# Moving work between VectorE, ScalarE and GpSimd in a macaron block with a chunked delta-rule attention, under a new order of instructions

## The chip, the cores and the metric

The kernel runs on one core of a Trainium2 chip. The time is the device time of one execution in microseconds, from the start of the program to its end; lower is better. The engines are TensorE (PE; PEld is its weight load), VectorE (DVE), ScalarE (ACT), GpSimd (POOL) and SyncE (SP), which issues the DMAs.

## The reference

The input x has 8 sequences of 256 rows and 256 channels. Three residual steps are applied to it:

```python
x = x + 0.5 * ffn(layernorm(x))
x = x + attn(layernorm(x))
x = x + 0.5 * ffn(layernorm(x))
```

The feed-forward part is a gated unit of 1024 with Hadamard transforms, which the kernel folds into the weights. The attention has 16 heads, each with a key and value width of 128. For every row there are one query and R = 4 key/value pairs, taken from projections that run through a causal convolution of 4 taps and a SiLU; q and k are normalized; a decay per row and channel comes from a softplus (G is its running sum). The sequence is cut into chunks with a state S of 128x128 carried from one to the next:

```python
w = beta * k
M[t,i; s,m] = sum_d k[t,i] * exp(G[t] - G[s]) * w[s,m]     # strictly lower triangular
rhs = v - (k * exp(G)) @ S
u = solve(I + M, rhs)                                        # unit diagonal
o = SCALE * (q * exp(G) @ S + tril(q * exp(G[t] - G[s]) @ w) @ u)
S = exp(G_last) * S + (w * exp(G_last - G)).T @ u
...
out = (o * rsqrt(mean(o**2) + eps) * onorm_w * sigmoid(gate)) @ Wo.T
```

## The kernel before

There are three stages: the first feed-forward with the gate inputs, the attention, and the output projection with the second feed-forward. Nearly all of the time is the attention stage, and all of the change is there but for a constant.

The attention stage works on 64 groups: 4 pairs of sequences (bp; the two sequences of a pair are b = 0 and 1) times 16 heads, in this order. The kernel uses chunks of C = 32 rows, 8 for each sequence. The steps of one group:

- `proj` (L946): nine projections of 128x512 (one for q, four for k, four for v). Each is six matmuls in TensorE; ScalarE writes the last convolution tap into kr or vr, and VectorE adds the other three. In the 16 groups of bp = 0 the weights are also split into high and low parts (wblk, a cast on ScalarE, a subtraction on GpSimd) and stored; later groups fetch them (w_d).
- `silu_k` (L1012) writes kq (SiLU, 128x1280 for each b) and copies the keys into k4; `silu_v` (L998) writes v4 (SiLU, 128x1024 for each b) and sig (Tanh).
- `gates` (L1025): the softplus (za, zm: Abs, Relu, Exp, Ln on ScalarE), the scan cs on VectorE, then the decays of five levels in el: subtractions on GpSimd, one Exp on ScalarE for each b. Level lv serves pairs of blocks of 2^lv rows. ek, eg, qh and nq come from the same scan.
- `m_piece` (L1094), four pieces pc for each group: the products of keys and decays (l0, l1, ls2 to ls4 for the columns, lt1 to lt4 for the rows), then 160 small matmuls into a PSUM tile mt for each half piece, from which N (ScalarE) and at (VectorE) are read.
- `inverse` (L1187): the 32x32 diagonal blocks of N go to DRAM (nd) and come back, one block for each partition (nl); GpSimd solves all columns at once in 31 steps of a product (ltmp) and a sum (yl). nk, the norms of the keys, is a square root: a power on GpSimd. The result goes through DRAM (yd) into Yt.
- `double` (L1238) makes 128x128 inverses of the 32x32 ones: VectorE transposes blocks (Xt), a 32-row step (p32, copy ps1, y32), and a 64-row step (p64, copy ps2, y64, copy into Yt).
- `recur` (L1385): for 8 chunks and both sequences p_r (TensorE), rt (VectorE), p_u (TensorE), u (copy), p_s (TensorE), S (VectorE), with ke, kd, kdT, vN prepared by `recur_prep` (L1304).
- `post` (L1400): rs, the reciprocal root for the normalization, a power on GpSimd; the scaling of o, its transposes, the product with sig and the store.

**The order.** Every operation is recorded first. `arrange` (L402) then sorts the operations of all groups by group x period + a position that the table ROUND (L41) holds for the operation's kind and number; each engine gets its instructions in that order, once and for all. Positions of one group reach from about -100 to 190 while the period is 68.814, so a round of the machine holds work of four groups: the projections of a later one, the pieces of the next, the inverse, and the recurrence of an earlier one. A position modulo the period gives the place in a round. BUFS (L37) has the number of buffers for each tile, ENG (L39) the engine of each copy and product (v VectorE, g GpSimd, s ScalarE), one letter for each instance.

**Tables of ScalarE.** `act` (L226) names the table set that a function needs. While `arrange` goes through the order, it puts in a table load wherever an operation needs another set than the last one: SILU_SET for v4, sig (Tanh) and kq, EXP_SET for the Exp and Ln of za, el and ek. Copies, Abs, Relu, Square and scalings name none.

**Fillers.** `keep_warm` (L582) puts matmuls on constants (L1454, into a spare part of mt) into planned gaps of TensorE, as long as the planned busy share of the last 3.4 us is below BUSY.

Of the kernel before, what the change touches and what calls it, by code (L numbers as in the profile page):

```python
# [20 lines left out]
P = 128  # L21
# [15 lines left out]
BUFS = {'kr': 1, 'vr': 1, 'kq': 2, 'v4': 4, 'k4': 5, 'N': 8, 'at': 9, 'ek': 4, 'eg': 6, 'qh': 4, 'wblk': 2, 'w2': 1, 'sm': 3, 'cl': 2, 'nk': 3, 'nq': 16, 'sig': 3, 'so': 24, 'rs': 21, 'ke': 3, 'kd': 1, 'vN': 2, 'kdT': 3, 'u': 8, 'S': 8, 'rt': 2, 'ps2': 1, 'wraw': 2, 'f_h': 8, 'raw': 3, 'ohl': 3, 'x4': 1, 'f_xhl': 1, 'ln_xn': 1, 'xhl': 1, 'fg': 1, 'be': 1, 'za': 1, 'zm': 1, 'el': 1, 'q2': 2, 'l0': 1, 'lt1': 1, 'lt2': 1, 'ls2': 1, 'lt3': 1, 'ls3': 1, 'lt4': 1, 'ls4': 2, 'nl': 1, 'sw': 1, 'yl': 1, 'ltmp': 1, 'ps1': 1, 'o': 1}  # L37

ENG = {'l0': 'vvvv', 'l1': 'vvvg', 'lt1': 'vvvv', 'lt2': 'gvvv', 'lt3': 'vvvv', 'lt4': 'vvvv', 'ls2': 'vvvv', 'ls3': 'vvvv', 'ls4': 'vvvv', 'ke': 'vvvvvvvv', 'kd': 'vvvvvvvv', 'qh': 'vv', 'k4': 'ss', 'zm': 'v', 'nl': 'v', 'el': 'gggggggggg', 'ek': 'gg', 'N': 'ssssssss', 'u': 'ssssssssssssvsss', 'vN': 'ssssssssssssssss', 'kdT': 'ssssssss', 'ps1': 'ssss', 'ps2': 'ss', 'X32': 'ss', 'Y32': 'ssss', 'Y64': 'ss', 'o': 'ssss', 'on': 'ssss', 'nk': 's', 'eg': 'ss', 'wh': 's', 'at': 'vvvvvvvv', 'tap': 'vvvvvvvvv'}  # L39

ROUND = {"period": 68.814, "at": {  # L41
    'gp:ek': [11.377, 12.737],
    'gp:el': [-25.595, -25.712, -24.539, -25.433, -23.461, -25.598, -23.752, -23.755, -25.592, -23.755, 9.204, 4.916, 8.065, 5.102, 6.615, 4.377, 9.811, 4.773, 10.026, 10.591],
    'gp:l1_1': [28.618],
    'gp:lt2': [-22.399],
    'gp:ltmp': [48.887, 51.825, 53.362, 54.257, 54.649, 56.717, 61.287, 62.202, 64.383, 64.837, 66.74, 67.664, 69.55, 73.202, 73.876, 76.049, 78.203, 78.703, 79.577, 81.108, 81.477, 85.569, 88.294, 89.684, 90.649, 91.459, 91.894, 93.63, 93.767, 96.173, 96.359],
    'gp:nk': [98.248],
    'gp:rs': [173.727],
    'gp:wblk': [-90.104, -89.629, -67.446, -59.41, -57.936, -40.937, -38.162, -32.75, -28.503],
    'gp:yl': [34.532, 47.962, 48.222, 49.996, 52.065, 53.571, 54.563, 55.066, 60.271, 61.711, 63.621, 64.509, 66.1, 67.039, 68.097, 71.874, 73.69, 74.124, 76.947, 78.452, 79.147, 79.975, 81.426, 85.281, 85.934, 89.07, 90.329, 91.062, 91.866, 93.407, 93.652, 95.846, 96.181, 96.554],  # L50
    'sc:N': [-6.953, -7.892, 11.221, 16.582, 21.323, 26.437, 31.718, 35.019],
    'sc:Xt0': [113.673],
    'sc:Xt1': [113.782],
    'sc:Yt0': [115.328, 114.885, 117.841],
    'sc:Yt1': [115.453, 115.214, 118.518],
    'sc:eg': [86.088, 108.103],
    'sc:ek': [17.438, 13.205, 17.438, 17.441],
    'sc:el': [-23.061, 10.712],
    'sc:k4': [-25.428, 9.155],
    'sc:kdT': [97.137, 101.186, 129.746, 130.662, 140.024, 143.13, 151.489, 157.263],  # L60
    'sc:kq': [-31.991, -31.802],
    'sc:kr': [-68.822, -62.007, -59.973, -50.065, -48.956],
    'sc:nk': [67.803],
    'sc:o': [147.184, 143.199, 151.16, 165.94, 165.972, 167.312, 176.914, 178.906, 176.92, 176.569],
    'sc:ps1': [110.606, 110.094],
    'sc:ps2': [115.551, 117.509],
    'sc:q2': [-10.36, 22.442],
    'sc:sig': [26.085],
    'sc:u': [119.942, 123.611, 127.068, 129.495, 136.818, 138.35, 141.509, 141.948, 146.735, 147.631, 149.124, 154.215, 161.784, 165.023, 165.068],
    'sc:v4': [27.91, 28.253],  # L70
    'sc:vN': [100.738, 100.735, 101.434, 101.213, 127.78, 127.071, 129.587, 130.228, 141.392, 141.576, 141.945, 142.52, 150.948, 156.786, 156.382, 155.345],
    'sc:vr': [-34.884, -28.219, -27.02, -20.568],
    'sc:wblk': [-91.119, -90.691, -67.582, -64.336, -59.106, -49.023, -40.507, -35.493, -28.927],
    'sc:za': [-33.996, -31.044, -30.853],
    'sc:zm': [-34.081],
    'sy:Yt0': [105.729, 107.105, 104.757, 107.387],
    'sy:Yt1': [103.524, 106.806, 103.662, 107.727],
    'sy:be': [44.808, -20.372],
    'sy:fgl': [-45.079],
    'sy:nd': [4.23, 16.805, 16.828, 17.812, 18.974, 19.369, 22.319, 27.202, 30.032, 30.711, 32.382, 34.581, 36.972, 38.357, 40.801, 41.422],  # L80
    'sy:nl': [43.757, 43.901],
    'sy:o': [186.894],
    'sy:w': [-89.684, -87.074, -66.467, -51.713, -42.051, -38.245, -35.074, -25.824, -26.322],
    'sy:w2': [-41.765],
    'sy:wblk': [-93.367, -89.838, -67.181, -66.47, -52.1, -43.986, -38.28, -30.869, -30.06],
    'sy:wraw': [-92.729, -91.457, -89.183, -87.864, -65.109, -49.447, -41.511, -37.744, -30.244],
    'sy:xhl': [-93.404],
    'sy:yd': [99.135, 100.159],
    'te:mt0': [-10.644, 0, 0, 0, 0, 0, 0, 0, 0, 0, 0, 0, 0, 0, 0, 0, 0, 0, 0, 0, 0, 0, 0, 0, 0, 0, 0, 0, 0, 0, 0, 0, 0, 0, 0, 0, 0, 0, 0, 0, 0, 0, 0, 0, 0, 0, 0, 0, 9.442, 0, 0, 0, 0, 0, 0, 0, 0, 0, 0, 0, 0, 0, 0, 0, 0, 0, 0, 0, 0, 0, 0, 0, 0, 0, 0, 0, 0, 0, 0, 0, 0, 0, 0, 0, 0, 0, 0, 0, 0, 0, 0, 0, 0, 0, 0, 0, 19.694, 0, 0, 0, 0, 0, 0, 0, 0, 0, 0, 0, 0, 0, 0, 0, 0, 0, 0, 0, 0, 0, 0, 0, 0, 0, 0, 0, 0, 0, 0, 0, 0, 0, 0, 0, 0, 0, 0, 0, 0, 0, 0, 0, 0, 0, 0, 0, 28.864],
    'te:mt1': [-17.993, 0, 0, 0, 0, 0, 0, 0, 0, 0, 0, 0, 0, 0, 0, 0, 0, 0, 0, 0, 0, 0, 0, 0, 0, 0, 0, 0, 0, 0, 0, 0, 0, 0, 0, 0, 0, 0, 0, 0, 0, 0, 0, 0, 0, 0, 0, 0, 11.4, 0, 0, 0, 0, 0, 0, 0, 0, 0, 0, 0, 0, 0, 0, 0, 0, 0, 0, 0, 0, 0, 0, 0, 0, 0, 0, 0, 0, 0, 0, 0, 0, 0, 0, 0, 0, 0, 0, 0, 0, 0, 0, 0, 0, 0, 0, 0, 24.906, 0, 0, 0, 0, 0, 0, 0, 0, 0, 0, 0, 0, 0, 0, 0, 0, 0, 0, 0, 0, 0, 0, 0, 0, 0, 0, 0, 0, 0, 0, 0, 0, 0, 0, 0, 0, 0, 0, 0, 0, 0, 0, 0, 0, 0, 0, 0, 34.527],  # L90
    'te:p32': [108.88],
    'te:p64': [115.408, 0, 0, 0, 0, 0, 0, 0, 116.095],
    'te:p_ot': [179.18],
    'te:p_r': [124.617, 126.108, 133.994, 136.571, 139.4, 140.262, 144.848, 145.843, 148.38, 148.537, 156.119, 157.599, 162.507, 162.792],
    'te:p_s': [122.138, 123.878, 127.286, 130.259, 137.699, 139.056, 142.425, 143.6, 147.291, 148.063, 149.938, 156.545, 158.406, 162.504],
    'te:p_u': [119.002, 121.356, 126.433, 127.195, 136.764, 137.598, 140.805, 141.927, 146.259, 147.258, 148.54, 152.195, 157.045, 159.754, 163.073, 164.034],
    'te:pgate': [22.588],
    'te:pn': [67.727],
    'te:po': [142.529, 0, 0, 0, 0, 0, 0, 0, 0, 0, 0, 0, 0, 0, 165.6],
    'te:pproj': [-76.39, 0, 0, -70.897, 0, 0, -67.676, 0, 0, -66.718, 0, 0, -61.594, 0, 0, -60.722, 0, 0, -57.959, 0, 0, -54.182, 0, 0, -49.585, 0, 0, -49.501, 0, 0, -37.337, 0, 0, -35.82, 0, 0, -32.624, 0, 0, -31.701, 0, 0, -29.108, 0, 0, -27.327, 0, 0, -25.906, 0, 0, -25.514],  # L100
    'te:pq': [37.003, 38.263, 37.124, 37.775],
    'te:pv': [90.502, 0, 94.616, 0, 101.112, 0, 101.115, 0, 125.899, 0, 122.248, 0, 118.999, 0, 126.094, 0, 137.287, 0, 137.412, 0, 141.79, 0, 141.625, 0, 148.543, 0, 148.383, 155.095, 0, 152.784],
    'te:pz': [-35.014],
    'te:y32': [111.675],
    'te:y64': [117.131, 0, 0, 0, 0, 0, 0, 0, 117.578],
    've:S': [123.037, 124.889, 130.671, 134.218, 138.442, 139.928, 142.468, 145.226, 147.734, 148.401, 152.826, 156.972, 158.65, 162.627],
    've:Xt0': [107.37, 111.673, 106.836],
    've:Xt1': [105.404, 111.622, 106.244],
    've:at': [0.188, 3.648, 19.324, 19.334, 20.927, 28.353, 42.532, 42.462],
    've:cl': [46.296, 46.593],  # L110
    've:cs': [-29.476],
    've:kd': [90.977, 97.203, 105.267, 124.194, 128.516, 138.134, 144.363, 148.513],
# [7 lines left out]
    've:ls4': [-23.029, -11.997, 13.582, 21.025],  # L120
    've:lt1': [-21.795, -8.666, 19.293, 26.201],
    've:lt2': [-1.993, 19.19, 26.204],
    've:lt3': [-21.792, -5.389, 19.261, 26.774],
    've:lt4': [-22.417, 0.248, 19.314, 27.204],
    've:nl': [46.988],
    've:nq': [39.479],
# [1469 lines left out]
```

## Time and profile before

| | |
|---|---|
| median of 3 runs | 4800.92 us (4788.68 to 4819.71) |
| profiled execution | 4781.15 us, span 4779.4 us |
| granted TensorE clock, mean | 0.951 |
| busy: PE, DVE, ACT, POOL | 4197.5, 3828.0, 3156.2, 3019.2 us |
| first and last scan cs | 272.9 and 4348.1 us |
| DMA | 351.13 MB, mean 73 GB/s |

All instructions of the attention stage are recorded by one helper (L623), so the profile's groups are told apart by the tiles that they write and read and by shapes. "l_g" is l0, "l" is l1, "ls_g" ls2 to ls4, "lt_g" lt1 to lt4, "k_g" k4, "v_g" v4, "ps_g" ps1 and ps2, "p_g" p32 and p64, "y_g" y32 and y64. Durations in a group are means; the idle time in front of a group is put down to what ended it.

### The profile page before, as it was taken

How to read it: one execution, taken by the hardware profiler on the slowest of the kernel's cores; microseconds unless marked ns; L12 is line 12 of the kernel's file. 1: busy time of each engine (PE TensorE's matmuls, PEld its weight loads, DVE VectorE, ACT ScalarE, POOL GpSimd, SP SyncE). 2: the span in 40 equal slices, each digit the busy share in tenths (PEclk: the TensorE clock that was granted, in tenths of full speed). 3: DMA queues.
4: the chain of work that ended last, by engine and by line, in shares of the span. 5: the costliest groups of instructions: out<-in, count | busy, mean ns of one | idle time of the engine just before them, and what ended most of it. 6: DMA issues, size and time to landing. Idle time of an engine off the chain costs nothing.

```text
span 4779.4 us, 197459 instructions
## 1 busy us (share of the span) xinstructions
PE 4197.5 (88%) x83786; PEld 3450.4 (72%) x83786; DVE 3828.0 (80%) x8811; ACT 3156.2 (66%) x7152; POOL 3019.2 (63%) x6090
## 2 busy tenths in 40 slices
PE   8878888888888888888888888888988888888799
PEld 5767777777777777777777777777777777777688
DVE  4368888888888888888988889888889988887333
ACT  3247766776777776777777767777777777776332
POOL 4257776777766667666666676666667766666321
PEclk9989999898999999999999999999999999999899
DMA  3133222322322322223323222223322222222421
GB/s 129 59 103 82 80 74 80 85 71 76 93 75 67 71 61 63 66 67 71 82 68 71 61 64 66 67 68 75 77 61 65 70 65 68 68 66 46 128 85 45
DMA packets 607651, 351.13 MB, mean 73 GB/s; under 512 B 439472, under 2 KB 510896, under 8 KB 605360
## 3 DMA queue, kind: packets, MB, share of 16 engines
q1 hardware_dynamic: 606768, 338.50, 27.6%
q8 instruction: 659, 10.80, 0.9%
q14 instruction: 224, 1.84, 0.1%
HBM read 232.94 MB, written 105.38 MB: 71 GB/s over the span
## 4 chain that ended last, share of the span: by engine, by line
DVE 42%; PE 32%; ACT 13%; DMA 5%; issue 4%; POOL 3%; SPq 1%; POOLq 0%; DVEq 0%; ACTq 0%
DVE kr_g L623 10%; DVE lt_g L623 5%; ACT v_g L623 5%; PE pproj_g L623 4%; DVE S_g L623 4%; PE mt L623 3%; PE p_g L623 3%; DVE ke_g L623 3%; DVE vr_g L623 3%; DVE ls_g L623 3%; DVE rt_g L623 3%; PE y_g L623 3%; PE mt L1454 3%; DMA wblk_g<-w_d 2%; DVE l_g L623 2%
## 5 line engine op out<-in xcount | busy, mean ns | idle before, releaser
L623 PE MATMUL pproj_g<-xhl_g,wblk_g 128*128 128x512 f32 x3456 | 1087.3, 434 | 151.7 <-DMA wblk_g<-w_d 74.1
L623 POOL TENSOR_TENSOR yl_g<-yl_g,ltmp_g 128x126 f32<-128x126 f32 (+22 forms) x1984 | 899.2, 453 | 127.4
L623 POOL TENSOR_TENSOR ltmp_g<-yl_g,nl_g 128x126 f32<-128x126 f32 (+22 forms) x1984 | 815.1, 411 | 121.3 <-POOL yl_g L623 0.3
L623 POOL TENSOR_TENSOR el_g<-cs_g 128x128 f32<-128x128 f32 x1280 | 513.6, 421 | 461.6 <-DVE nq_g L623 437.8
L623 PEld LDWEIGHTS pproj_g<-xhl_g,wblk_g 128*128 128x128 f32 x3456 | 603.4, 197 | 274.0 <-DVE Xt L623 45.8
L623 DVE SCALAR_TENSOR_TENSOR kr_g<-pproj_g,small,kr_g 128x510 f32<-128x510 f32 (+2 forms) x960 | 701.7, 737 | 18.9 <-ACT kr_g L623 15.5
L623 DVE SCALAR_TENSOR_TENSOR vr_g<-pproj_g,small,vr_g 128x510 f32<-128x510 f32 (+2 forms) x768 | 554.2, 735 | 158.6 <-ACT vr_g L623 151.9
L623 ACT COPY u_g<-p_u_g 128x128 f32<-128x128 f32 x960 | 255.7, 266 | 419.0 <-PE p_u_g L623 413.2
L623 DVE TENSOR_TENSOR lt_g<-kq_g,el_g 128x320 f32<-128x320 f32 x960 | 527.3, 580 | 0.0
L623 PE MATMUL mt<-lt_g,ls_g 128*16 128x20 f32 (+2 forms) x16384 | 500.8, 205 | 9.1 <-DVE ls_g L623 1.1
L623 PE MATMUL p_r_g<-S_g,ke_g 128*128 128x128 f32 x1792 | 392.9, 301 | 67.4 <-DVE S_g L623 60.2
L623 ACT ACTIVATE vN_g<-pv_g,nk_g 128x128 f32<-128x128 f32 x1024 | 355.5, 373 | 89.2 <-DVE rt_g L623 80.7
L623 PEld LDWEIGHTS p_r_g<-S_g,ke_g 128*128 128x128 f32 x1792 | 278.5, 189 | 151.4 <-DVE S_g L623 58.4
L623 PE MATMUL p_s_g<-u_g,kdT_g 128*128 128x128 f32 x1792 | 374.9, 291 | 14.5 <-ACT u_g L623 6.7
L623 PE MATMUL p_u_g<-rt_g,Yt 128*128 128x128 f32 x1792 | 373.6, 290 | 12.1 <-DVE rt_g L623 4.4
L623 DVE TENSOR_TENSOR ls_g<-k_g,el_g 128x256 f32<-128x256 f32 x768 | 356.8, 465 | 21.6 <-ACT el_g L623 15.9
L623 PEld LDWEIGHTS p_s_g<-u_g,kdT_g 128*128 128x128 f32 x1792 | 286.7, 192 | 98.1 <-issue 42.0
L623 PE MATMUL mt<-kq_g,k_g 128*32 128x20 f32 x8192 | 308.4, 193 | 38.5 <-DVE at_g L623 38.5
L623 ACT ACTIVATE kr_g<-pproj_g,small 128x512 f32<-128x512 f32 x320 | 219.9, 687 | 160.7 <-PE pproj_g L623 160.7
L623 PEld LDWEIGHTS mt<-lt_g,ls_g 128*16 128x16 f32 (+1 forms) x16384 | 313.7, 102 | 16.5 <-DVE ls_g L623 16.2
L623 PEld LDWEIGHTS p_u_g<-rt_g,Yt 128*128 128x128 f32 x1792 | 273.6, 190 | 68.3 <-DVE rt_g L623 32.7
L623 PEld LDWEIGHTS mt<-kq_g,k_g 128*32 128x32 f32 x8192 | 211.5, 109 | 146.6 <-issue 63.4
(170 smaller groups left out, 10773.4 us busy)
## 6 DMA issues: line engine op xcount, KB each, us to landing
wblk_g<-w_d SPq DMA_DIRECT2D x432, 256.0 KB, 2.9
w_d<-wblk_g SPq DMA_DIRECT2D x144, 256.0 KB, 2.1
nl_g<-nd_g SPq DMA_DIRECT2D x128, 256.0 KB, 4.1
wraw_g<-in_wa_dram SPq DMA_DIRECT2D x144, 128.0 KB, 2.4
nd_g<-N_g SPq DMA_DIRECT2D x1024, 16.0 KB, 2.2
yd_g<-yl_g SPq DMA_DIRECT2D x128, 128.0 KB, 3.5
Yt<-yd_g SPq DMA_DIRECT2D x512, 32.0 KB, 2.0
o_d<-sig_g SPq DMA_DIRECT2D x64, 256.0 KB, 3.3
```

Source lines behind the costliest of these rows:

```text
L623: getattr(getattr(self.nc, o["e"]), o["m"])(*o["a"], **o["k"])
L1454: nc.tensor.matmul(mts[b][:, TG - P:], ident, ident, start=True, stop=True)
```

## The change

- The square root of nk and the reciprocal root rs are made by ScalarE: Ln, then Exp with a scale of 0.5 or -0.5, both of EXP_SET. The powers on GpSimd and their constant pos_half go.
- The first decay level (one row against the next) is kept for the first row of each pair only: el shrinks from 5 x 256 to 128 + 4 x 256 columns, GpSimd does one subtraction in place of two, l0 multiplies every other row (128x256 in place of 128x512) and copies the others on ScalarE (l0c).
- ENG: ls3 of three pieces and ls4 of all four go from VectorE to GpSimd; lt2 of one piece comes back; the one u copy on VectorE goes to ScalarE.
- The 64-row step of `double`: in place of both p64 bursts, then both y64 bursts, it runs p64 of b=0, then p64 of b=1 and y64 of b=0 matmul by matmul in turn, then y64 of b=1. The two use different row and column halves of the array (tile positions (0, 64) and (64, 0)).
- All positions in ROUND are new, the period is the same. Some costs of the planner change, among them BUSY for the fillers, 0.55 to 0.65. Some tiles have other buffer counts.

```diff
-BUFS = {... 'at': 9 ... 'sm': 3 ... 'nq': 16 ... 'so': 24, 'rs': 21 ... 'kd': 1 ... 'sw': 1 ...}
+BUFS = {... 'at': 8 ... 'sm': 1 ... 'nq': 11 ... 'so': 1, 'rs': 17 ... 'kd': 2 ... 'sw': 2 ...}
-ENG = {... 'lt2': 'gvvv' ... 'ls3': 'vvvv' ... 'ls4': 'vvvv' ... 'u': 'ssssssssssssvsss' ...}
+ENG = {... 'lt2': 'vvvv' ... 'ls3': 'gggv' ... 'ls4': 'gggg' ... 'u': 'ssssssssssssssss' ... 'l0c': 'ssss'}
...
-    BUSY = 0.55
+    BUSY = 0.65
...
-            el = s1.tile([P, 5, T], F32, tag="el", name="el")
-            for lv in range(5):
+            el = s1.tile([P, T // 2 + 4 * T], F32, tag="el", name="el")
+            pairs = csb.rearrange("p (n two) -> p n two", two=2)
+            tt("el", 0, el[:, 0:T // 2], pairs[:, :, 0], pairs[:, :, 1], op=ALU.subtract)
+            for lv in range(1, 5):
...
-        tt("l0", pc, l0, k4, el[:, 0, e0:e0 + P].unsqueeze(2).to_broadcast([P, P, R]), op=ALU.mult)
+        l0p, k4p = l0.rearrange("p (a e) r -> p a e r", e=2), k4.rearrange("p (a e) r -> p a e r", e=2)
+        tt("l0", pc, l0p[:, :, 0], k4p[:, :, 0], el[:, e0 // 2:(e0 + P) // 2].unsqueeze(2).to_broadcast([P, P // 2, R]),
+           op=ALU.mult)
+        copy("l0c", pc, l0p[:, :, 1], k4p[:, :, 1])
...
-        copy("nk", 0, nk, pn)
+        pl.act(EXP_SET, nk, pn, AF.Ln)
+        pl.act(EXP_SET, nk, nk, AF.Exp, scale=0.5)
...
-        pl.record("gpsimd", "tensor_tensor", (nk, nk, pos_half), {"op": ALU.pow}, cost=2.9)
...
+        for step in range(SB + 1):
...
             for j in range(NCH):
+                for args, kw, c in ([up(step, j, step > 0)] if step < SB else []) + ([down(step - 1, j, step < SB)] if step else []):
+                    pl.record("tensor", "matmul", args, kw, cost=c)
             pl.burst(i0)
+            if step < SB:
+                ps2.append(s1.tile([P, NCH, 64], F32, tag="ps2", name="ps2"))
+                copy("ps2", step, ps2[step][64:128], p3[step][64:128])
...
-        pl.record("gpsimd", "tensor_tensor", (rs, rs, neg_half[:, 0:4]), {"op": ALU.pow}, cost=1.8)
+        pl.act(EXP_SET, rs, rs, AF.Ln)
+        pl.act(EXP_SET, rs, rs, AF.Exp, scale=-0.5)
```

`up` is the p64 matmul and `down` the y64 matmul, as they were. Of the new positions in ROUND, these are the ones of ScalarE that name a table set (and, for place, u):

```diff
-    'sc:v4': [27.91, 28.253],
-    'sc:sig': [26.085],
-    'sc:kq': [-31.991, -31.802],
-    'sc:za': [-33.996, -31.044, -30.853],
-    'sc:el': [-23.061, 10.712],
-    'sc:ek': [17.438, 13.205, 17.438, 17.441],
-    'sc:u': [119.942, 123.611, 127.068, 129.495, 136.818, 138.35, 141.509, 141.948, 146.735, 147.631, 149.124, 154.215, 161.784, 165.023, 165.068],
+    'sc:v4': [16.329, 27.01],
+    'sc:sig': [28.613],
+    'sc:kq': [-37.157, -36.562],
+    'sc:za': [-38.117, -37.602, -37.359],
+    'sc:el': [-32.63, 12.031],
+    'sc:ek': [8.859, 30.255, 29.254, 30.266],
+    'sc:nk': [68.538, 76.854],
+    'sc:rs': [167.553, 167.555],
+    'sc:u': [115.744, 116.787, 126.627, 129.974, 134.51, 136.758, 140.928, 140.984, 145.578, 145.833, 152.431, 153.882, 157.269, 162.113, 166.244, 166.303],
```

## The prediction

> **What bounds it now.** The execution shown took 4781.15 us, its span 4779.4; the median of the runs is 4800.92. I sum against 4781.15 and add the difference, 19.8, at the end. First the engines' shares and the chain that ended last, from the page:
>
> ```profile
> PE 4197.5 (88%) x83786; PEld 3450.4 (72%) x83786; DVE 3828.0 (80%) x8811; ACT 3156.2 (66%) x7152; POOL 3019.2 (63%) x6090
> DVE 42%; PE 32%; ACT 13%; DMA 5%; issue 4%; POOL 3%; SPq 1%; POOLq 0%; DVEq 0%; ACTq 0%
> ```
>
> VectorE has the largest part of the chain, though TensorE shows more busy time; TensorE's ends are modelled, and 296.2 us of it are filler matmuls (L1454). Then the stages. The scan that writes cs runs once for each of the 64 groups, from 272.9 us to 4348.1: 63 rounds. The first 15 (weights split on the way, to 1281.5) average 67.2 us, the other 48 63.9. The windows (columns: length, then busy time and instructions of PE, PEld, DVE, ACT, POOL, then clock, DMA share, GB/s):
>
> ```profile
> 273.00:1180.00 907.00, 786.35 (x16358) 642.66 (x16358) 754.29 (x1676) 618.47 (x1417) 646.72 (x1287) 0.91 0.29 79
> 1180.00:4348.00 3168.00, 2818.28 (x62614) 2302.82 (x62613) 2789.58 (x6537) 2301.46 (x5268) 2145.65 (x4516) 0.97 0.29 69
> ```
>
> In the second row DVE is busy 88.1%, that is 56.3 us of a 63.9 us round; ACT 46.4, POOL 43.3. So DVE works 56.3 us and stands idle 7.6. The waits over those 48 rounds (us in total, times, longest) say why:
>
> ```profile
> DVE vr_g L623 <- ACT vr_g L623: 117.2, 48, 2.5
> DVE zm_g L623 <- ACT za_g L623: 112.3, 48, 2.4
> DVE at_g L623 <- PE mt L1454: 74.2, 47, 3.6
> ```
>
> That is 2.4 + 2.3 + 1.5 = 6.3 of the 7.6. Both ACT waits lie in one stretch; the timelines of ACT and of DVE around it:
>
> ```profile
> 2532.97 1.28 ACT L623 ACT_TABLE_LOAD   x1
> 2534.26 0.69 ACT L623 ACTIVATE sig_g<-pgate_g,bg2h 128x512 f32<-128x512 f32 x1
> ...
> 2537.05 4.00 ACT L623 ACTIVATE v_g<-vr_g 128x1024 f32<-128x1024 f32 x2
> ...
> 2548.59 1.28 ACT L623 ACT_TABLE_LOAD   x1
> 2549.88 1.29 ACT L623 ACTIVATE za_g<-za_g 128x512 f32<-128x512 f32 x2
> ```
> ```profile
> 2544.43 0.75 DVE L623 SCALAR_TENSOR_TENSOR vr_g<-pproj_g,small,vr_g 128x510 f32<-128x510 f32 x1 [2.47 <-ACT vr_g L623]
> 2551.21 0.69 DVE L623 TENSOR_TENSOR zm_g<-zm_g,za_g 128x512 f32<-128x512 f32 x1 [2.36 <-ACT za_g L623]
> ```
>
> The two v4 SiLUs (4.0 us), then the two kq SiLUs and a table load hold up what DVE needs next. A round is about 30 us of DVE back to back, then a half in which DVE, ACT and PE hand over to each other.
>
> **The parts.** Rows used (columns: count | busy us, mean ns | idle before):
>
> ```profile
> L623 DVE TENSOR_TENSOR lt_g<-kq_g,el_g 128x320 f32<-128x320 f32 x960 | 527.3, 580 | 0.0
> L623 DVE TENSOR_TENSOR ls_g<-k_g,el_g 128x256 f32<-128x256 f32 x768 | 356.8, 465 | 21.6 <-ACT el_g L623 15.9 <-PE mt L623 3.4
> L623 DVE TENSOR_TENSOR l_g<-k_g,el_g 128x512 f32<-128x512 f32 x256 | 204.8, 800 | 0.0
> L623 DVE TENSOR_TENSOR l<-k_g,el_g 128x256 f32<-128x256 f32 x192 | 93.7, 488 | 0.0
> L623 POOL TENSOR_TENSOR nk_g<-nk_g,pos_half 128x16 f32<-128x16 f32 x64 | 201.6, 3150 | 0.0
> L623 POOL TENSOR_TENSOR rs_g<-rs_g,neg_half 128x4 f32<-128x4 f32 x64 | 65.0, 1016 | 38.9 <-DVE rs_g L623 38.8
> L623 POOL TENSOR_TENSOR l<-k_g,el_g 128x256 f32<-128x256 f32 x64 | 51.9, 812 | 0.0
> ```
>
> VectorE, per round. On DVE an instruction's duration overlaps the next one's start by 0.08 us (an ls of 0.42 us at 2508.10 is followed at 2508.43), so each counts 0.08 less. Seven products go to GpSimd (three ls3, four ls4): 7 x 0.385 = 2.70. The four l0 halve from 512 to 256 elements, 0.800 to 0.488 (the l1 row, as strided as the new l0): 1.25. One u copy goes to ACT: 0.274 - 0.08 = 0.19. One lt2 comes back: 0.58 - 0.08 = 0.50. Net -3.64. With the shortest rows (ls 0.406, l0 0.675) it is -3.0; I take the means, since moved and remaining products still run beside GpSimd.
>
> GpSimd loses the roots (3.15 + 1.02), two 0.42 subtractions of the first level and an lt2 of 0.81, together 5.8; it gains seven products at 0.81, the one row of that shape, 5.7. Even, on an engine with 20 idle us; but three products (2.4 us, where one lt2 of 0.81 stood) now run ahead of the column recursion in yl, and three more inside it. What is late next is yd, Yt, then the Xt transposes. Cover: the recursion ended at 2535.4, yd (3.5) and Yt (2.0) put the blocks down near 2541, the first Xt ran at 2545.76; DVE waited for Yt only 13.6 us in the whole run. Counted 0; 1.6 + 2.4 us with the cover gone.
>
> The Trainium skill, "SBUF — State Buffer", section "SBUF: two separate sides", says that a VectorE product with two SBUF inputs and a GpSimd instruction reading SBUF exclude each other for a whole instruction. By that rule alone the seven moved products (5.7 us) could come off DVE's time again, 2.70 saved against 5.7 lost. The rows show milder: l0 has median 0.680 and mean 0.800, ls 0.418 and 0.465, with GpSimd busy two thirds of the time, and that busy time does not grow.
>
> ScalarE gains: four l0 copies of 128x256 (the kdT copy is 0.384, the weight cast 0.412; overlap 0.09): 1.3; the u copy 0.17; Ln and Exp for both roots in place of one nk copy, three small instructions more at about 0.2 less overlap: 0.3; the el exponentials are 128 columns shorter, twice, at 1.07 ns: -0.27. **And table loads**: sorting the new ACT positions modulo the period, v4 (16.3, 27.0) and sig (28.6) are followed by Exp on ek and by rs and za, then kq SiLUs (31.7, 32.3), then el. That alternates twice: four loads a round where there were two (133 in all before), 2 x 1.283 = 2.57. Sum +4.1, ACT 46.4 to 50.5.
>
> The Trainium skill, "ScalarE: Activation LUTs", section "Table sets: the hidden batching unit", says to do all of one set before the other, and its section "What ACT_TABLE_LOAD costs" puts a switch at 2.66 us, a drain included. That speaks against this order. The trace has 1.28 and no gap around it: load at 2548.59, next Exp at 2549.88. By the page ACT would gain 6.9 us a round, by the row 4.1.
>
> Does it land? I walked ACT in the new order with durations from the timelines, less overlap. Before, from u.14 (2536.24) to the end of el for b=0 (2558.50) took 22.3 us. New, from the same u.14: two u, N, vN 1.0; load 1.3, ek 0.45; three squares and copies of o with an l0 copy 1.3; roots, waiting for DVE's rs, 0.6; kdT, two vN, two scalings of o 1.4; two ek and N 1.2; vr.0 0.6 (7.9 so far); two scalings, za and zm with Exp and Ln, N 3.3 (za ready at 10.9); load and kq 3.9; two ps1 and vr.1 1.8; load, vr.2 and el 3.2: 20.0, and 21.5 with k4 behind it. Three loads stand in it instead of one, but the v4 SiLUs are out of it, and za and zm stand ahead of kq. DVE's waits in there, walked the same way: rs 0.6, vr.0 1.4, zm 0.5, vr.3 1.7, vr.6 0.5 = 4.7, against 2.47 + 2.36 + 0.99 (at) = 5.8: -1.1. What pays is the recurrence: v4.0 with its load and neighbours puts 4.0 us between u.11 and u.12, v4.1 with neighbours 4.3 between u.13 and u.14. In the trace these u copies are 5.4 (2525.48 to 2530.94) and 3.6 (2532.68 to 2536.24) us apart, behind DVE's queue. Late by 0.7, and by more as DVE's part shrinks: I take +1.3 (between 0 and 8.3). S, rt and all taps behind them on DVE would wait.
>
> The 64-row steps: each step is 8 x 0.12 = 0.94 us. Chain now: up for b=0, copy ps2, down, copy, down; the second up already lies beside the first copy. Alternated, the chain keeps its five links, TensorE saves up to 0.94 beside a copy: 0. Nor do I count the higher filler share (0.55 to 0.65): 4.6 us of fillers a round, 18% more is +0.8; fewer half-clock stretches could give -1.4 (63.9 to the quickest round, 62.5). The new DMA order: TensorE waits 74.1 us for wblk in 48 rounds, 1.5 each; between -1.5 and +1.5, taken 0.
>
> **Sum.** -3.64 - 1.1 + 1.3 = -3.4 a round. For 49 rounds 167 us; in the 15 with weight splitting, where ACT and POOL carry nine more instructions each, half: 25. 4781 - 192 + 20 = **4609 us**. Its own range, from -3.0 + 1.3 and -3.64 - 1.1 - 1.4 per round: 4705 down to 4455.
>
> **Rivals.** (A) The early SiLUs hold the recurrence: slower. Place: v4.0 with its load before u.12, v4.1 before u.14. Price up to 8.3 us a round; it decides from 4.4 (3.64 saved, and 0.75 to pass 1%). At 6.5: +2.9 a round, 4781 + 186 + 20 = 4987. For: static order, S and rt behind u on DVE. Against: the 5.4 and 3.6 us that are there already. 0.09. (B) ACT's 4.1 us land in full, since ACT already ends both large DVE waits: -3.64 + 4.1 = +0.5, 4830, no change. Against: ACT still idles 13 us. 0.12. (C) ACT's new order is worth more: DVE at 52.7 and half its idle, 3.8: 56.5 us a round, -7.4 x 49 - 3.7 x 15 = -418, 4383. For: both ACT waits are what the order attacks. Against: the load before el, and TensorE, 56.8 us less 4.6 of fillers, comes to 52.2. 0.14. That the alternating steps do not run at once is possible too, but hidden: 0.
>
> Forecast 0.65. About 1% (48 us) is what a measurement here can tell from no change. Faster by over 1%: 0.65 + 0.14 = 0.79; within 1% 0.12 (B); slower 0.09 (A). The range takes in B and half of C: 4430 to 4830.
>
> **What would show it.** DVE near 53 busy us a round and POOL still near 43; some 260 table loads of 1.28 us, ACT near 50; no pow on POOL; DVE waits on vr and zm smaller, a new one on vr behind kq and the loads. Wrong if u copies 12 and 14 spread further apart (A), if DVE's idle time grows past 11 us a round (B), or if Xt waits for Yt.

## The result, and the profile after

The changed kernel takes **4832.47 us** (median; 4821.55 to 4853.74) beside 4800.16 us for the kernel before on the same chip: a ratio of 1.0072, 95% interval 1.0056 to 1.0088. It is slower by 0.7%, where 4609 was forecast. That lies within 1%, the case that had 0.12, and 2.5 us past the upper end of the range.

The profiled execution has a span of 4833.9 us. From its page, the engines and the chain that ended last:

```profile
PE 4236.4 (88%) x84624; PEld 3490.5 (72%) x84624; DVE 3837.7 (79%) x8363; ACT 3381.0 (70%) x7793; POOL 2886.0 (60%) x6217
PE 35%; DVE 34%; ACT 22%; issue 3%; DMA 3%; POOL 2%; SPq 1%; ACTq 0%; POOLq 0%; DVEq 0%
```

DVE has 448 instructions fewer than before and the same busy time (3828.0 before). ACT's share of the chain went from 13% to 22%. From scan to scan the first 15 rounds take 67.2 us as before; the other 48 take 65.07, before 63.89. Those 48 x 1.18 = 57 us are the whole difference of the two spans (54.5). One row for these 48 rounds (length, busy time and instructions of PE, PEld, DVE, ACT, POOL, then clock, DMA share, GB/s):

```profile
1275.00:4398.30 3123.30, 2776.11 (x61150) 2276.03 (x61150) 2696.62 (x6001) 2383.47 (x5569) 1974.72 (x4465) 0.98 0.28 67
```

Per round DVE is busy 56.2 us (before 56.25, forecast near 53), ACT 49.7 (before 46.3), and DVE stands idle 8.9 (before 7.6). Its waits in these rounds:

```profile
DVE S_g L620 <- PE p_s_g L620: 178.0, 144, 3.3
DVE vr_g L620 <- ACT vr_g L620: 119.2, 96, 1.8
DVE lt_g L620 <- PE mt L620: 49.6, 48, 1.0
DVE at_g L620 <- PE mt L1461: 28.1, 32, 1.2
```

The wait of zm for za (112.3 before) is gone, as the walk said. The one on vr is as long as it was, in two pieces, and S in the recurrence waits 178.0 us (34.1 before), up to 3.3 at once. Most of it lies at two places. The first S behind u.0 waits 1.83 us a round, behind the stage shown under "Where ACT's time went". A later S, between the two v4 SiLUs, waits 1.47 us a round:

```profile
2555.50 0.35 DVE L620 SCALAR_TENSOR_TENSOR S_g<-S_g,eg_g,p_s_g 128x128 f32<-128x128 f32 x1 [1.47 <-PE p_s_g L620]
```

Its u was copied at 2553.76, but TensorE had a gate projection (pgate, 1.12 us from 2553.89) and a p_u ahead of p_s. What S waits for there is TensorE's order, not ScalarE.

**Where the products' time went.** Rows of DVE, POOL and ACT (count | busy us, mean ns of one):

```profile
L620 DVE TENSOR_TENSOR lt_g<-kq_g,el_g 128x320 f32<-128x320 f32 x1024 | 628.8, 634 | 74.7 <-PE mt L620 72.2
L620 DVE TENSOR_TENSOR ls_g<-k_g,el_g 128x256 f32<-128x256 f32 x320 | 193.4, 604 | 0.0
L620 DVE TENSOR_TENSOR l_g<-k_g,el_g 128x256 f32<-128x256 f32 x256 | 155.7, 608 | 0.0
L620 DVE TENSOR_TENSOR l<-k_g,el_g 128x256 f32<-128x256 f32 x192 | 130.2, 678 | 8.0 <-ACT el_g L620 7.9
```
```profile
L620 POOL TENSOR_TENSOR ls_g<-k_g,el_g 128x256 f32<-128x256 f32 x448 | 337.2, 763 | 391.4 <-issue 234.8 <-PE mt L620 86.3 <-ACT k_g L620 70.2
```
```profile
L620 ACT ACT_TABLE_LOAD x262 | 336.1, 1283 | 5.3 <-PEq L1588 0.7
```

Every remaining product got longer: lt 580 to 634 ns, ls 465 to 604, l1 488 to 678, and the halved l0 took 608 where I put 488. The timelines of DVE and POOL show why (start, duration):

```profile
2518.37 0.85 DVE L620 TENSOR_TENSOR l_g<-k_g,el_g 128x256 f32<-128x256 f32 x1
2519.14 0.85 DVE L620 TENSOR_TENSOR l<-k_g,el_g 128x256 f32<-128x256 f32 x1
2519.92 0.41 DVE L620 TENSOR_TENSOR ls_g<-k_g,el_g 128x256 f32<-128x256 f32 x1
```
```profile
2517.44 2.28 POOL L620 TENSOR_TENSOR ls_g<-k_g,el_g 128x256 f32<-128x256 f32 x3 [4.92 <-issue]
2519.66 0.52 POOL L620 MEMSET yl_g<- 128x512 f32 x1
```

Products of one size: 0.85 us while POOL has its three ls (to 2519.72), 0.41 after them, beside a MEMSET, which writes and reads nothing. The two long ones come out so in all 48 rounds, the short one in 45.

**Where ACT's time went.** The stage from the scan cs to the first u copy of the recurrence, one window a round, first of the kernel before, then two of the changed kernel:

```profile
2489.47:2502.12 12.65, 11.26 (x209) 9.64 (x211) 12.31 (x25) 10.20 (x20) 7.79 (x19) 1.00 0.36 105
```
```profile
2507.85:2523.56 15.71, 13.66 (x263) 11.41 (x263) 13.45 (x23) 14.20 (x23) 8.29 (x17) 1.00 0.39 96
2571.62:2588.82 17.20, 15.18 (x263) 12.79 (x263) 13.54 (x23) 14.17 (x22) 9.40 (x22) 0.90 0.35 87
```

At full clock the stage grew from 12.65 to 15.71 us, and ACT in it from 10.2 of 12.65 to 14.2 of 15.7. Where the granted clock falls (0.90), another 1.5 us come on top. Over the ten or eleven rounds from 2000 to 2700 us the stage has a mean of 13.6 us before and 16.6 after; the rest of the round went from 49.9 to 48.3. The rest of the round, which holds most of the products, is 1.6 us shorter, and this stage 3.0 longer. Not all of that is gain or loss: the two kq SiLUs (2.64 us) stood ahead of cs before (at 2545.94, cs at 2552.00) and stand behind it now. Nor is the falling clock new: before, the stage took 12.65 to 15.99 us at clocks from 1.00 to 0.70. ACT in it:

```profile
2506.57 1.28 ACT L620 ACT_TABLE_LOAD   x1
2507.87 2.64 ACT L620 ACTIVATE kq_g<-kr_g 128x1280 f32<-128x1280 f32 x2
...
2513.16 1.28 ACT L620 ACT_TABLE_LOAD   x1
2514.45 1.26 ACT L620 ACTIVATE el_g<-el_g,ea 128x1152 f32<-128x1152 f32 x1
2515.73 0.36 ACT L620 COPY Xt<-y_g 32x256 f32<-32x256 f32 x1
```

Two of the four loads stand here, one just before the stage and one in it, ahead of el and of the copies that the solve hands on.

### The profile page after: what moved, and what is told of

It is laid out like the page before. It is cut to its first block, busy times and chain, and to the rows that moved or that the text cites. A ratio compares the mean times of both kernels' runs of the same rounds, so it can differ in the third digit from the quotient of the medians.

```text
span 4833.9 us, 199466 instructions
## 1 busy us (share of the span) xinstructions
PE 4236.4 (88%) x84624; PEld 3490.5 (72%) x84624; DVE 3837.7 (79%) x8363; ACT 3381.0 (70%) x7793; POOL 2886.0 (60%) x6217
## 4 chain that ended last, share of the span: by engine, by line
PE 35%; DVE 34%; ACT 22%; issue 3%; DMA 3%; POOL 2%; SPq 1%; ACTq 0%; POOLq 0%; DVEq 0%
DVE kr_g L620 8%; DVE lt_g L620 8%; PE mt L620 5%; DVE ke_g L620 3%; PE y_g L620 3%; PE pproj_g L620 3%; PE p_u_g L620 3%; ACT kq_g L620 3%; ACT L620 3%; DVE kd_g L620 3%; PE p_r_g L620 3%; DVE ls_g L620 3%; DVE S_g L620 3%; PE mt L1461 2%; PE p_s_g L620 2%
## 5 line engine op out<-in xcount | busy, mean ns | idle before, releaser
L620 PE MATMUL pproj_g<-xhl_g,wblk_g 128*128 128x512 f32 x3456 | 1048.2, 424 | 37.9 <-DVE vr_g L620 15.1
L620 POOL TENSOR_TENSOR yl_g<-yl_g,ltmp_g 128x126 f32<-128x126 f32 (+22 forms) x1984 | 825.5, 416 | 128.6
L620 POOL TENSOR_TENSOR el_g<-cs_g 128x128 f32<-128x128 f32 x1152 | 464.3, 422 | 698.2 <-DVE cs_g L620 633.5
L620 POOL TENSOR_TENSOR ltmp_g<-yl_g,nl_g 128x126 f32<-128x126 f32 (+22 forms) x1984 | 793.1, 400 | 120.0
L620 DVE SCALAR_TENSOR_TENSOR kr_g<-pproj_g,small,kr_g 128x510 f32<-128x510 f32 (+2 forms) x960 | 705.0, 735 | 15.7 <-ACT kr_g L620 14.5
L620 DVE TENSOR_TENSOR lt_g<-kq_g,el_g 128x320 f32<-128x320 f32 x1024 | 628.8, 634 | 74.7 <-PE mt L620 72.2
L620 POOL TENSOR_TENSOR ls_g<-k_g,el_g 128x256 f32<-128x256 f32 x448 | 337.2, 763 | 391.4 <-issue 234.8
L1461 PE MATMUL mt<-consts 128*128 128x128 f32 x2576 | 435.8, 300 | 0.0
L1461 PEld LDWEIGHTS mt<-consts 128*128 128x128 f32 x2576 | 378.9, 207 | 32.3 <-issue 0.9
L620 DVE SCALAR_TENSOR_TENSOR S_g<-S_g,eg_g,p_s_g 128x128 f32<-128x128 f32 x768 | 259.0, 337 | 132.8 <-PE p_s_g L620 128.8
L620 PE MATMUL p_g<-Xt,N_g 32*32 32x32 f32 x6144 | 271.0, 210 | 101.2 <-ACT ps_g L620 72.9
```

Of the source, the lines that this page charges most:

```text
L620: getattr(getattr(self.nc, o["e"]), o["m"])(*o["a"], **o["k"])
L1461: nc.tensor.matmul(mts[b][:, TG - P:], ident, ident, start=True, stop=True)
```

## The experiments

All ratios are to the kernel before, run on the same chip. "Round" is the mean of rounds 16 to 63 from scan to scan; the changed kernel has 65.07.

### GpSimd's products (theory: the two engines exclude each other)

**e1**: the changed kernel with the seven products back on VectorE, at the places that GpSimd's had.

```diff
-'ls3': 'gggv', 'ls4': 'gggg'
+'ls3': 'vvvv', 'ls4': 'vvvv'
+ROUND["at"]["ve:ls3"] = ROUND["at"]["gp:ls3"] + ROUND["at"]["ve:ls3"]
+ROUND["at"]["ve:ls4"] = ROUND["at"]["gp:ls4"]
```

> The changed kernel with all seven ls3 and ls4 products on VectorE again, at the places in the order that GpSimd had them. Theory 'exclusion' (VectorE's saving was eaten because its two-input products wait while a GpSimd product runs: 0.85 us beside one, 0.41 alone): VectorE takes 7 x 0.385 = 2.7 us back, but its other products fall to their short times, so its busy time stays within 1 us of 56.2 a round and the time stays within 4780 to 4850. Rival 'plain move' (the move did save VectorE 2.7 us and the time was lost elsewhere): VectorE about 59 us a round, time near 4832 + 64 x 2 = 4960.

Measured 4891.33 us, ratio 1.0179 (1.0142 to 1.0217), round 66.24. DVE is busy 54.5 us a round: with seven instructions more it works 1.7 us less, and its other products are short again (lt 543 ns for 634, l0 467 for 608). But its idle time grew from 8.9 to 11.7; one new wait is most of that:

```profile
DVE ls_g L622 <- ACT el_g L622: 100.1, 48, 2.1
```

That is 2.1 of the 2.8 us a round, an artefact of the places: GpSimd could wait there for el, VectorE can't without holding its queue. So busy time speaks for the exclusion, by more than I had expected; the whole time lies between the two expectations and decides nothing.

**e2**: GpSimd's seven products are left out; it writes constants at the same places in its order and reads nothing.

```diff
-                tt(f"ls{lv}", pc, lk[lv]..., halves(k4, hb)[:, :, 0], by_row(el_h(lv, 0), hb), op=ALU.mult)
+                if ENG[f"ls{lv}"][pc] == "g":
+                    pl.gpsimd.memset(lk[lv], 0.01)
+                else:
+                    tt(f"ls{lv}", pc, ...)
```

> The changed kernel, in which GpSimd writes a constant into the seven ls tiles in place of the product (the product is left out; nothing is read). Theory 'exclusion by reading': lt, l0, l1 and ls on VectorE near 0.42 to 0.50 (lt 0.63, l0 0.58, l1 0.67, ls 0.60 now), VectorE's busy time 53 to 54 us a round, time 4680 to 4760. Rival 'the length of the products is GpSimd's own affair': VectorE's rows stay, time within 30 us of 4832 but for GpSimd being about 3 us shorter.

Measured 4758.2 us, ratio 0.9908 (0.9886 to 0.993), round 63.78. Rows of DVE:

```profile
L620 DVE TENSOR_TENSOR lt_g<-kq_g,el_g 128x320 f32<-128x320 f32 x1024 | 554.5, 561 | 72.9 <-PE mt L620 68.9 <-ACT el_g L620 1.4
L620 DVE TENSOR_TENSOR l_g<-k_g,el_g 128x256 f32<-128x256 f32 x256 | 122.7, 479 | 0.0
```

lt 634 to 561 ns, l0 608 to 479, and DVE is busy 52.84 us a round. My sum had 56.3 - 3.64 = 52.7. So the sum of VectorE's busy time was right without the products beside it, and they take 3.3 us of it back, of 5.3 us that POOL spends on them (337.2 / 64). The memsets are also shorter than the products (313 ns for 763) and wait for neither k4 nor el, so e2 prices the products, not their reading alone; for the reading speaks the ls of 0.41 us beside a MEMSET, above. They free POOL of 2.9 us, so a part of the time's gain may be POOL's.

The round is only 1.29 us shorter for 3.3 us less of busy time: VectorE's idle time grew from 8.9 to 10.9 us. What it no longer works it mostly waits.

**e8**: the move alone, on the kernel before, in its own order.

```diff
-'ls3': 'vvvv', 'ls4': 'vvvv'
+'ls3': 'gggv', 'ls4': 'gggg'
+ROUND["at"]["gp:ls3"] = ROUND["at"]["ve:ls3"][:3]
+ROUND["at"]["ve:ls3"] = ROUND["at"]["ve:ls3"][3:]
+ROUND["at"]["gp:ls4"] = ROUND["at"]["ve:ls4"]
```

> The kernel before in its own order, with the seven ls3 and ls4 products on GpSimd, at the places that VectorE had for them. Exclusion: VectorE gives away 2.7 us a round and gets at least as much back in waits beside the products, busy 56 to 58, and GpSimd's column recursion gets 5.7 us longer: 4800 to 4900. Plain move: VectorE 53.5, 4640 to 4720.

Measured 4920.26 us, ratio 1.0282 (1.0244 to 1.032), slower than either expectation had it. DVE is busy 55.0 us a round, between the two: it lost 1.2 of the 2.7 us that the seven products had, POOL gained 5.6. The chain of this run lies on POOL:

```profile
POOL 41%; PE 28%; ACT 8%; DVE 7%; issue 7%; DMA 6%; SPq 2%; POOLq 0%; ACTq 0%; DVEq 0%
```

### The table loads (theory: they lie on the path)

**e3**: kq with Exp in place of SiLU (the SiLU of q and k is left out), all places as they are; two loads of the four go.

```diff
-            pl.act(SILU_SET, kq..., AF.Silu)
+            pl.act(EXP_SET, kq..., AF.Exp)
```

> The changed kernel with Exp of the other set in place of the two kq SiLUs (the SiLU of q and k is left out), so that two of the four table loads of a round go and nothing else. Theory 'loads on the path' (ScalarE's stretch from vr to k4 is gap-free and ends the chain): both loads come off in full, 2 x 1.28 x 64 = 164, time 4650 to 4700. Rival 'loads beside VectorE's queue': under 40 us, time 4790 to 4830.

Measured 4689.22 us, ratio 0.9762 (0.974 to 0.9784), round 62.76: 2.31 us less for 2.57 us of loads. The stage from cs to u.0 in this run:

```profile
2493.09:2506.99 13.90, 12.97 (x259) 10.74 (x259) 12.89 (x23) 11.38 (x19) 7.67 (x16) 1.00 0.44 107
```

In the 48 rounds it takes 13.9 to 14.3 us, and the clock in it stays 1.00. In the changed kernel it took 15.5 to 18.5, at clocks from 1.00 to 0.80. Over all 48 rounds the lost clock (1 less the granted, times the length) is 1.60 us a round in the changed kernel and 0.71 here. So of the 2.31 us up to 0.89 is clock. That the clock falls because TensorE idles behind the loads is my reading; no run sets the two apart. The kernel before loses 2.07 us a round, so the clock is not why the changed kernel is slower than that one.

**e5**: e2 and e3 together.

> Both of the last two together in the changed kernel: GpSimd writes constants in place of its seven ls products, and kq takes Exp of the other set, so two loads a round. If the forecast's sum was right but for two terms (exclusion, loads on the path), their corrections add: 4832 - 74 - 143 = 4615, near the 4609 of the forecast; VectorE 53 us busy a round. If one hides behind the other, 4680 or more, as with the loads alone.

Measured 4609.94 us, ratio 0.9625 (0.9607 to 0.9643), round 61.57. The two gains, 74 and 143 us, add up: 4832 - 217 = 4615. With both terms taken out, the forecast's time stands there to a microsecond. That is luck, for the parts do not agree. The 48 late rounds are 2.3 us shorter than in the kernel before, where the sum had 3.4; the first 15 are 3.6 shorter, where it had half of 3.4. VectorE works 3.4 us less a round, but stands idle 1.0 us more, where the sum had 0.2 more. And 0.07 us of clock are lost in a round here, 2.07 in the kernel before, which the sum took at 0.

**c1, c5, c8, c10**: can the two loads go with the whole computation? Four orders with two loads, each mended by the trace of the one ahead of it. The first:

```diff
+A = ROUND["at"]
+A.update({"gp:ek": [13.5, 15.8], "sc:ek": [8.859, 16.1, 16.15, 16.2], "sc:za": [-38.117, -36.55, -36.54], "sc:zm": [-36.545],
+          "ve:zm": [-36.3], "ve:cs": [-36.0], "sc:rs": [169.94, 169.945], "te:p_ot": [170.2],
+          "sc:o": A["sc:o"][:6] + [169.95, 169.96, 169.97, 169.98]})
```

> The changed kernel with all its work, but with ScalarE's order mended so that no step of the exp and ln set stands between the first SiLU of v4 and the last of kq: the exponentials of ek go before v4, exp and ln of the gate (za), the sum zm and the scan cs go behind kq, the root rs and the scalings of o behind them. Two table loads a round instead of four. Theory (two loads of 1.28 us lie on the path of each round): about 4690 us, 4660 to 4740, ScalarE busy near 47 us a round; the same gain as with kq's function exchanged (4689), here with the whole computation. Rival (the gate behind kq makes scan, el and the level products late, so what the loads gave is lost again): 4790 or more, with VectorE's waits for the el exponential grown.

Measured 5407.97 us, ratio 1.1266 (1.1241 to 1.1292). In the 48 rounds ScalarE waited 348.9 us in 96 places for GpSimd's ek, and TensorE's output transposes (p_ot) stood ahead of p32. Second, ek's places mended:

```diff
+          "sc:ek": [8.859, 32.28, 16.2, 32.285], "sc:el": [-31.714, 12.031]   # gp:ek as in the changed kernel
```

> The kernel with two loads again, with two places mended after the first try's trace: ScalarE stood 3.6 us twice a round for GpSimd's ek, which I had put ahead of its own work. Here GpSimd's ek stays where the changed kernel has it, only the one exponential of ek that the next product needs goes ahead of v4, the two others behind kq; and el's exponential goes behind the first copies of Xt and Yt, since the scan now comes some 2.4 us later. Theory (two loads of 1.28 us on the path, against a scan that is late by 2.4 us but has VectorE's other work beside it): 4690 to 4800 us, ScalarE's waits for GpSimd's ek gone. Rival (the scan behind kq is what cost the first try its time): above 4832, with VectorE and GpSimd waiting for cs and el.

Measured 5234.5 us, ratio 1.0902 (1.0869 to 1.0935). One line of ACT's timeline says what is left: 3.7 us before ps1, for a p32 that stands behind p_ot on TensorE.

```profile
2512.43 0.58 ACT L632 COPY ps_g<-p_g 32x512 f32<-32x512 f32 x1 [3.71 <-PE p_g L632]
```

Third, the output behind the first two u, and zm and cs behind three transposes of Xt:

```diff
+          "sc:ek": [8.859, 48.0, 16.2, 48.01], "ve:zm": [-35.79], "ve:cs": [-35.78], "sc:rs": [185.65, 185.66],
+          "sc:o": A["sc:o"][:6] + [185.67, 185.68, 185.69, 185.70], "te:p_ot": [187.6], "ve:sig": [188.0]
```

> Two loads, third order. The trace of the second try shows what cost it its time: the transposes of the output (p_ot) stood on TensorE behind ScalarE's scalings of o and ahead of p32, so that p32 came 3.7 us late, and VectorE stood 3.8 us a round for the gate (za) with a transpose for Xt behind it. Here the root rs, the scalings of o, p_ot and the sig product go behind the first two u of the recurrence, where ScalarE waits 2.7 us for TensorE anyway, together with the two exponentials of ek that the next round needs; zm and cs go behind the first three transposes of Xt. Theory (two loads of 1.28 us are on the path and can be taken off): 4640 to 4760 us. Rival (the gate behind kq costs what the loads gave, whatever stands around it): 4810 or more.

Measured 5107.56 us, ratio 1.0656 (1.0607 to 1.0705). The stage from cs to u.0 was down to 11.4 us in most rounds, but VectorE now stood for the output at the head of the recurrence:

```profile
2525.45 0.69 DVE L633 SCALAR_TENSOR_TENSOR sig_g<-sig_g,p_ot_g 128x512 f32<-128x512 f32 x1 [3.16 <-PE p_ot_g L633]
```

Fourth:

```diff
+          "sc:kq": [-38.62, -38.61], "sc:za": [-38.117, -37.59, -37.58], "ve:qh": [29.938, 29.95],
+          "sc:ek": [8.859, 58.0, 16.2, 58.01], "te:p_ot": [194.13], "ve:sig": [194.93]
+BUFS["kq"] = 3
```

> Two loads, last order. The trace of the third try shows its two remaining losses: u.2 came 5.0 us later after u.0 than in the changed kernel (8.6 against 3.6), because VectorE stood 3.2 us for the output transposes ahead of the state's update; and ScalarE stood some 3.9 us ahead of kq, for N, za and vr, where the changed kernel does its exponentials. Here p_ot and its product go behind the first p_r, the two late exponentials of ek behind u.2, and kq goes up into that gap (a third buffer of kq, qh earlier), ahead of the last N; the gate's exp and ln follow it at once. Theory (the order was the loss, and the loads can be taken off): 69.5 - 5.0 - 2.0 = 62.5 us a round, 4680 us, 4620 to 4780. Rival (what the order gains at one place a queue loses at another, as in the three tries): 4810 or more.

Measured 4950.86 us, ratio 1.0322 (1.0285 to 1.0359). Its waits show the next place:

```profile
ACT kq_g L636 <- DVE kr_g L636: 156.0, 47, 3.3
DVE vr_g L636 <- ACT vr_g L636: 147.1, 48, 3.2
```

kq was ahead of its taps, ScalarE stood for VectorE with vr behind it, and VectorE then for vr. From cs to u.0 this run takes 13.6 us (16.6 in the changed kernel), the rest of the round 53.3 (48.3). The rival was right in all four: what an order gained at one place, a queue lost at another. Whether some order has two loads and keeps the rest stays open. What e3 shows is the price of the loads in this order; no run shows that a better order was at hand.

**c9**: the third of these, with the seven products on VectorE beside their piece's; **c2**: the same on the first.

```diff
+          "ve:ls3": [-27.985, 3.45, 16.65, 29.367], "ve:ls4": [-27.783, 3.46, 16.95, 29.5]   # ENG as in e1
```

> The same, and the seven level products ls are back on VectorE, at places beside the other level products of their piece (not at GpSimd's early places, as in the run that put them back first). Theory (the move buys no VectorE time, since the two engines exclude each other): VectorE busy 54 to 55 us a round against 56, and the time 4630 to 4700, at or below the kernel with two loads. Rival (the move to GpSimd is worth what its seven products took, and the first run that put them back was slow for that): 1.5% or more above the kernel with two loads, 4760 and up.

> The same, with the seven level products ls back on VectorE, beside the other products of their piece. Theory (the two engines exclude each other, the move to GpSimd buys no VectorE time): within 1% of the same kernel with the products on GpSimd or below it, VectorE busy 54 to 55 us a round against 56. Rival (the products are worth their 2.7 us on GpSimd): 1.5% or more above it.

c2: 5419.63 us, ratio 1.1303 (1.1271 to 1.1336), 0.2% above c1. c9: 5169.46 us, ratio 1.0767 (1.0743 to 1.079), 1.2% above c8, a little more than I had allowed. DVE is busy 54.9 and 55.0 us a round, by 0.9 us less in c9 than in c8 and as much as in c1. So with the products on GpSimd the kernel is up to 1.2% faster here (the 0.2% are within the noise), though no busy time of VectorE is saved; in the kernel before's order (e8) the move cost 2.8%. Where the 1.2% come from is not shown. The clock is a candidate: c9 loses 3.96 us of it a round, c8 1.48, and c9's round is 1.4 us longer.

### The other parts, on the kernel before

**e6**: the half of the first level (the el and l0 hunks of the change; GpSimd's places of el without two, `"sc:l0": [-19.0, 2.2, 13.95, 27.7]`). **e7**: the roots by ScalarE (the nk and rs hunks). **c7**: e6 with the alternating 64-row steps.

> The kernel before in its own order, with the first-level part alone: el 128 columns shorter, l0 multiplied for every other row, the other rows copied by ScalarE. Theory 'VectorE's row sets the round where ScalarE adds no load': VectorE 56.25 to about 55 us a round, time 4720 to 4770. Rival 'ScalarE's copies, which wait for the product before them, land in its full stretch': 4800 to 4850.

> The kernel before in its own order, with both roots by Ln and Exp on ScalarE, placed among the other Exp work so that two table loads a round remain; GpSimd's two powers (4.2 us a round) go. Theory: GpSimd had time to spare and the powers lay behind its last product, so nothing changes: 4790 to 4815. Rival 'the powers hold VectorE's products too': 20 us or more faster.

> The kernel before with two parts of the change: the first level's product on half the elements with ScalarE's copy of the other half (4770 us by itself), and the alternating 64-row steps. Theory (the alternation moves no work; only the clock can differ): 4750 to 4790. Rival (the alternation brings the first sequence's solve forward by one burst of about 1 us in each round): 4725 or less.

e6: 4770.24 us, ratio 0.9953 (0.9932 to 0.9973); DVE busy 54.81 a round, 1.44 less (I had 1.25), of which idle time took 1.3 back: the profiled round went from 63.89 to 63.78 us. With c7 below, which does not differ from it beyond the noise, it is the quickest kernel here with the whole computation, ahead of the kernel before and the changed one. e7: 4796.42 us, ratio 1.0006 (0.9989 to 1.0024): POOL loses 4.2 us a round and nothing moves, so the powers were hidden. c7: 4775.88 us, ratio 0.9948 (0.9927 to 0.9969), as e6: the steps alone are worth nothing there, as counted.

### Fillers, steps and the clock

**e4**: no filler matmuls in the changed kernel. **c3**: the kernel before with BUSY = 0.65. **c4**: the changed kernel with its 64-row steps undone (the hunk reversed, y64 of b=0 placed at 109.76). **c6**: c4 with BUSY = 0.70.

> The changed kernel without any filler matmul in the attention stage (they compute nothing that is used). Theory 'fillers on the path' (eight of them, 1.1 to 2.0 us, stand right before the last 64-row burst): -1 us a round, time 4750 to 4790, if the clock holds. Rival 'the clock pays': granted clock below 0.93, time 4830 to 4950.

> The kernel before, and only the share of filler matmuls (BUSY) raised from 0.55 to 0.65. I had counted this at nothing with a range of +0.8 to -1.4 us a round. Since taking all fillers from the changed kernel cost 187 us, I expect -0.2 to -0.8% (4760 to 4790), with the granted clock up from 0.951 to about 0.965. Rival (the added fillers stand in TensorE's way as much as they hold the clock): 4795 to 4830.

> The changed kernel with the 64-row steps of the two sequences as before: both up steps first, then both down steps, no matmuls of the two alternating. Counted at nothing in the sum: 4815 to 4850, within 0.4% of the changed kernel. Rival (the alternation is what holds the recurrence late, since the first sequence's end now shares its burst with the second's step): 4780 or less.

> The changed kernel with its 64-row steps undone, as in the run that took 5026 us, and with more filler matmuls (BUSY 0.70 for 0.65). In that run the granted clock fell to 0.50 for some 9 us of each round, just in these steps, where the changed kernel keeps 1.00, and two filler matmuls fewer stood before them. Theory (the loss was the clock, not the order of the steps): the clock comes back to 0.96 or more and the time to 4820 to 4880. Rival (the alternation itself is worth it): the clock comes back and the time stays above 4950. If the clock stays near 0.92 the run decides nothing.

e4: 5019.03 us, ratio 1.0446 (1.0427 to 1.0464): the rival's case, and past its range. Its mean clock:

```profile
core 0: 5021.1 us, clock 0.877
```

(0.964 in the changed kernel.) c3: 4811.8 us, ratio 1.0021 (1.0004 to 1.0038), clock 0.956: a miss, the rival's case. More fillers are worth nothing in the order before. c4: 5025.61 us, ratio 1.0468 (1.0451 to 1.0485), far from both expectations. The clock shows why; two windows with the second half of the 64-row steps, c4 and the changed kernel:

```profile
2552.00:2556.00 4.00, 4.00 (x37) 3.88 (x36) 2.74 (x7) 1.50 (x3) 2.64 (x7) 0.50 0.10 35
```
```profile
2520.00:2524.00 4.00, 3.97 (x60) 3.47 (x55) 3.07 (x8) 2.60 (x6) 2.65 (x7) 1.00 0.02 6
```

At half the clock TensorE's 4 us held 37 matmuls; the changed kernel's 4 us held 60. The last 16 y64 matmuls took 1.97 us in c4 and 1.14 there. In all 48 rounds c4 loses 5.1 us of clock a round, 3.5 more than the changed kernel, and its round is 3.2 longer (68.27). c6 took 4996.97 us, ratio 1.0407 (1.0375 to 1.0438), with the clock at 0.929: it didn't come back, so by its own terms the run decides nothing on whether the order of the steps or the fillers' places keep it up.

## Why the prediction was wrong

The sum had -3.4 us for a late round; it became 1.2 longer. Of the 4.6 us between them, 3.6 are VectorE's busy time (-3.64 forecast, -0.07 measured) and 1.05 its idle time (+0.2 forecast, +1.25 measured).

**The step that failed first: "that busy time does not grow".** I held -3.64 us a round on VectorE against the rule of the Trainium skill ("SBUF — State Buffer", section "SBUF: two separate sides") and chose the means of the rows before. The measured busy time fell by 0.07. The arithmetic was right (52.84 in e2 beside 52.7); what was wrong is the reading of the rows. A median of 0.418 beside a mean of 0.465 is better read as few products meeting a GpSimd instruction than as meetings that are cheap. Three of the moved products stand beside VectorE's own of the same piece (2517.44 to 2519.72 above). The rule held here (0.85 us beside a GpSimd product, 0.41 alone) and, as a sum, was too harsh: 5.7 us by it, 3.3 measured with e2.

**The second: "Does it land?".** I counted 2.57 us of loads in ACT's sum and let them vanish in a walk that ended at el. ACT grew by 3.3 us a round (4.1 counted), and e3 shows 2.31 us of the round behind the two loads. The walk compared the wrong ends: the path goes on over Xt, ps2 and Yt to u.0, and ACT is busy 14.2 of the 15.7 us from cs to u.0. The waits did not shrink by 1.1; DVE's idle time grew by 1.25. The Trainium skill's page "ScalarE: Activation LUTs", section "Table sets: the hidden batching unit", had spoken against this order, and e3 agrees. The 2.66 us that its section "What ACT_TABLE_LOAD costs" gives for a switch, a drain included, are not seen: the loads take 1.28 us without a gap, and the measurement decides.

**The third: busy time at full price.** The sum took each microsecond that VectorE no longer works off the round. Where the busy time did fall, most of it came back as idle time: 3.34 us less bought 1.29 us of the round in e2, 3.12 bought 1.19 in e5 beside e3, and 1.44 bought 0.1 in e6 (0.4 by the medians). So VectorE's row did not set the round by itself, and -3.64 would not have come in full without the exclusion either. Which waits took the place of the saved work is not followed further here.

**What was counted at nothing.** The roots (e7), the alternating steps on the kernel before (c7) and the later column solve (DVE waits 1.8 us for Yt's DMA in 48 rounds) were rightly 0. In the changed kernel the steps are not nothing: undone, they cost 193 us (c4), by the clock. The new DMA order took away TensorE's waits for wblk (74.1 us in 48 rounds before, 1.0 after); what that was worth is not shown. The l0 half was right in busy time by itself (-1.44 for -1.25). The higher BUSY was 0 in c3. The +1.3 for u behind the early SiLUs did not come in that way: both u copies after a v4 wait for TensorE (1.33 and 1.25 us), not for ScalarE. So rival A fell with it.

**The rivals.** The time is B's (4830), and B's mechanism is half of it: ACT's loads land. But B had kept the -3.64, and that term went to zero, while of ACT's 4.1 the 2.3 behind the loads landed. That B's number came out is luck. B's sign, DVE idle past 11 us, did not show (8.9). C needed shorter waits: zm's went, vr's stayed, and S's grew by 3.0 us a round (34.1 to 178.0 in 48). The clock, taken at 0 with a gain of up to 1.4 us, gave 0.5 us a round (2.07 lost before, 1.60 after).

## What to carry to other kernels

A product moved from VectorE to GpSimd saves VectorE's time only as far as VectorE's own two-input products do not stand beside it: count the time that both would read SBUF together, not the mean of a row that seldom met. Then ask how much of the saved time the round will give: here it gave about two fifths (e2), or less (e6). Sort a new ScalarE order by table set first, and follow its loads to the end of the path, not to the end of its own stretch. A trial that replaces the suspected cost at its place (a memset for a product, a function of the same set) prices it in one run, where reordering by hand moved four other queues.

## What was not expected of the hardware

The granted clock moves the time by as much as the whole change was to. Without fillers the mean clock went from 0.964 to 0.877 and the time up by 187 us; with the 64-row steps not alternating it fell to 0.50 in one stage, for 193 us; in the changed kernel a dip to 0.90 makes the same stage 1.5 us longer. While GpSimd ran three of its products one after the other, two VectorE products took 0.85 us each, twice the 0.41 of one of that size after them.
